# Rows of x instead of table rows for 48 edge tiles, edge lists read in rows, and expert tiles among the last blocks' and the last routing's products

## The chip, the cores and the metric

One Trainium2 chip, one core. Its engines run side by side, each with a queue of its own that is worked off in order: PE (TensorE, matrix products and transposes), DVE (VectorE), ACT (ScalarE), POOL (GpSimd, here almost only the issuer of indirect DMAs) and SP (SyncE, here only an issuer of DMAs). Sixteen DMA engines carry all transfers. The metric is the device time of one execution in microseconds (us); a program's time is the median of several. PE's clock is throttled: the profile shows the granted clock as a share of the full one.

## The reference

A graph layer with attention and then a layer of experts, over N = 6250 nodes of C = 256 numbers and 206,250 edges, sorted by destination. H = 8 heads of D = 32; 16 experts with a hidden layer of 512, two of them for each node.

```
hn    = layernorm(x)                       # no scale, no shift
hh    = (hn @ W).reshape(n, 8, 32)
s     = leaky_relu(<hh, a_src>[src] + <hh, a_dst>[dst])
alpha = softmax of s over the edges of one dst
out   = segment_sum(hh[src] * alpha, dst) + hn
x1    = x + elu(layernorm(out) * gamma + beta)
y     = layernorm(x1)
z     = y + sum over the top 2 of softmax(gate) * expert(y)   # relu, 256 -> 512 -> 256
x2    = x1 + layernorm(z) * gamma2 + beta2
```

Everything is float32 but for a few tables of scores in bfloat16.

## The kernel before

Nodes lie in NB = 49 blocks of 128. Edges lie in NK = 52 windows of CT = 31 tiles of 128 edges, 1612 tiles; a window is worked in four groups of 8, 8, 8 and 7 tiles (`GROUPS`), 208 groups.

**Preparation.** All of x is loaded into `xs` on SP (batches of 2, 6, 8, 8, ... blocks), then the first destination of each window (`base_i`) and the two edge lists `dst_i` and `src_sb`, in which a partition holds 31 successive edges of each window (124 bytes in a piece, `edge_list`, L129). For each block, statistics on DVE (`stats`, L193 and L194), two transposes on PE (L294) copied by ACT (L296), two passes of two products with `wx` (L299; the 256 columns of W and 16 of scores) into one of four PSUM buffers `ph`, and three activations (L302, L308, L309) make a row of R = 280 numbers for each node: eight heads of 32 with a 1 behind each, and 16 exponentials of scores. DVE copies the scores (L310), and the row goes to the DRAM tensor `table` by a DMA that POOL issues (L313). Ahead of batch 6, `windows()` (L242 to L282) makes each edge's destination relative to its window (`dl`), stores it as bytes in rows (`dlb`), and takes its largest and smallest (L271, L272).

**Main loop.** For each group, `gather` (L200) issues one indirect DMA on POOL for each tile (L205): 128 rows of the table by the sources in one column of `src_sb`, into one of four `hx` buffers. `look` (L1022, L1029, L1040) builds on DVE the one-hot matrices of the group one ahead and on PE the destinations' scores. DVE then weighs the rows (L1064, L1067, L1069 and L1072, the long one), and PE adds them up by destination into `agg` (L1076). At a window's end `agg` and a carry from the window before (L1093) are copied and stored to `accd`. When a block's edges are all in, `node_block` (called by `blocks`) reads it back, divides, normalises, and finds the two experts of each node, with PE's share at L623 and L628.

**Experts.** Blocks are routed in five rounds that end at 14, 26, 35, 43 and 49 blocks. `routing` (L634) counts and places the round's nodes and finds the expert of each tile of 128 rows (`owner`, L808). `scatter` (L817, L820, L830) sends each block's rows twice, by two indirect DMAs on POOL, from five buffers `ys`. The round's tiles (43, 39, 33, 31 and 27, together 173) then go through `stages()` (L976), one call per group: it takes a third tile's output (`rows_out`, L896, L898), a second's hidden layer (`hidden`, L881, L890), another's transposes (`turned`, L872, L874) and a next one's weights (`weights`, 512 KB each of w1 and w2 on SP). `some()` issues four scatters and one `stages()`.

**After the loop.** Three sets of buffers take result rows (`fetch_set`, L915), `blocks(summed)` runs the last two node blocks and the last routing, all left scatters go out, and a loop of `stages()` and `result` (L927 to L942) finishes the tiles and the output.

The order of work on each engine is the order in which the program issues it. `tc.issue_after(i)` adds that an instruction stands behind `i` where both are on one engine; across engines it adds nothing. The loop's core:

```
hx, gathered = early.pop(0) if early else gather(k, g0, n)
...
sums.append(t)
some()
if g0 == 0:
    blocks(summed)
    summed = []
```

Of the kernel before, what the change touches and what calls it, by code (L numbers as in the profile page):

```python
# [10 lines left out]
F32 = mybir.dt.float32  # L11
BF16 = mybir.dt.bfloat16
U8 = mybir.dt.uint8
I32 = mybir.dt.int32
# [22 lines left out]
def kernel(  # L37
# [89 lines left out]
    tp, tr = tail // CT, tail % CT  # L127

    def edge_list(eng, t, ap):  # L129
        eng.dma_start(  # L130
            t[:, : (NK - 1) * CT].rearrange("p (k g) -> p k g", g=CT),
            ap[0 : (NK - 1) * CE].rearrange("(k p g) -> p k g", p=P, g=CT),
        )
        o = (NK - 1) * CE
        if tp:
            eng.dma_start(t[:tp, (NK - 1) * CT : NT], ap[o : o + tp * CT].rearrange("(p g) -> p g", g=CT))
        if tr:
            eng.dma_start(
                t[tp : tp + 1, (NK - 1) * CT : (NK - 1) * CT + tr],
                ap[o + tp * CT : NE].rearrange("(p g) -> p g", p=1),  # L140
            )

    hxp = ctx.enter_context(tc.tile_pool(name="hxp", bufs=4))
    prep = ctx.enter_context(ExitStack())
    ed = prep.enter_context(tc.tile_pool(name="ed", bufs=1))
    dst_i = ed.tile([P, NT], I32, name="dst_i")
    nc.vector.memset(dst_i[:, (NK - 1) * CT :], N - 1)
    nc.vector.memset(src_sb[:, (NK - 1) * CT :], PADN)
    nc.vector.memset(src_sb[:, NT:], PADN)
    xs = ed.tile([P, NB, C], F32, name="xs")  # L150
    nc.vector.memset(xs[:, NB - 1, :], 0.0)
    batches = []
    while not batches or batches[-1][1] < NB:
        i = batches[-1][1] if batches else 0
        batches.append((i, min(NB, i + (2, 6, 8)[min(2, len(batches))])))
    for i, j in batches:
        n = min(j, NB - 1) - i
        if n:
            nc.sync.dma_start(xs[:, i : i + n, :], x[i * P : (i + n) * P, :].rearrange("(i p) c -> p i c", p=P))
    nc.sync.dma_start(xs[:LAST, NB - 1, :], x[(NB - 1) * P : N, :])  # L160
    wx = ed.tile([P, KC, C + 2 * H], F32, name="wx")
# [6 lines left out]
    nc.sync.dma_start(base_i[:, : NK - 1], dst[0 : (NK - 1) * CE].rearrange("(k e) -> e k", e=CE)[0:1, :])  # L168
    nc.sync.dma_start(base_i[:, NK - 1 :], dst[(NK - 1) * CE : (NK - 1) * CE + 1].rearrange("(k e) -> e k", e=1))
    edge_list(nc.sync, dst_i, dst)  # L170
    edge_list(nc.sync, src_sb, src)

# [5 lines left out]
    gg = row_of(g_gamma, C, "gg")  # L178
    gb = row_of(g_beta, C, "gb")
    fg = row_of(f_gamma, C, "fg")  # L180
    fb = row_of(f_beta, C, "fb")
    gtb = row_of(gate_b, E, "gtb")
    gw = const.tile([P, KC, E], F32, name="gw")
    nc.sync.dma_start(gw, gate_w.rearrange("(k p) e -> p k e", p=P))


    rest = const.tile([P, NB, C], F32, name="rest")
# [12 lines left out]
    def gather(k, g0, n):  # L200

        hx = hxp.tile([P, n, R], F32, name="hx")
        for g in range(n):
            c = k * CT + g0 + g
            t = nc.gpsimd.indirect_dma_start(  # L205
                out=hx[:, g, :],
                out_offset=None,
                in_=table[:, :],
                in_offset=bass.IndirectOffsetOnAxis(ap=src_sb[:, c : c + 1], axis=0),
            )  # L210
        return hx, t
# [5 lines left out]
    with tc.tile_pool(name="a1", bufs=1) as a1, tc.tile_pool(name="a3", bufs=3) as a3, tc.tile_pool(  # L217
        name="aps", bufs=4, space=bass.MemoryType.PSUM
    ) as aps:
# [22 lines left out]
        def windows():  # L242

            base_f = a1.tile([1, NK], F32, name="base_f")
            nc.vector.tensor_copy(base_f, base_i)
            bb = aps.tile([P, NK], F32, name="pxt")
            nc.tensor.matmul(bb, lhsT=ones[:1, :], rhs=base_f, start=True, stop=True)
            base_b = a1.tile([P, NK], F32, name="base_b")
            nc.vector.tensor_copy(base_b, bb)
            nc.vector.tensor_sub(down[:, : NK - 1], base_b[:, : NK - 1], base_b[:, 1:])  # L250
            nc.vector.tensor_copy(dl, dst_i)
            d3 = dl.rearrange("p (k g) -> p k g", g=CT)
            nc.vector.tensor_tensor(d3, d3, base_b[:, :, None].to_broadcast([P, NK, CT]), ALU.subtract)

            dlt = a1.tile([P, TR, P], U8, name="dlt")
            for i in range(TR):
                n = min(P, NT - i * P)
                pt = aps.tile([P, P], F32, name="pxt")
                nc.tensor.transpose(pt[:n, :], dl[:, i * P : i * P + n], ident)
                nc.scalar.copy(dlt[:n, i, :], pt[:n, :])  # L260
                nc.sync.dma_start(dlb[i * P : i * P + n, :], dlt[:n, i, :])
# [8 lines left out]
            two = a1.tile([P, 2], F32, name="two")  # L270
            nc.vector.tensor_reduce(two[:, 0:1], dl, AX.X, ALU.max)  # L271
            nc.vector.tensor_reduce(two[:, 1:2], dl, AX.X, ALU.min)  # L272
            nc.vector.tensor_scalar(two[:, 1:2], two[:, 1:2], -1.0, float(P - 1), op0=ALU.mult, op1=ALU.add)
            pw = aps.tile([2, P], F32, name="pxt")
            nc.tensor.transpose(pw, two, ident)
# [7 lines left out]

        for q, (i0, i1) in enumerate(batches):
            if q == 6:
                base_f, pf_ = windows()
            for b in range(i0, i1):
                stats(a3, xs[:, b, :], st[:, b, :])
            inv_std(rstd[:, i0:i1], st[:, i0:i1, 1])
            nc.vector.tensor_scalar_mul(low[:, i0:i1], rstd[:, i0:i1], 0.2)  # L290
            for b in range(i0, i1):
                pt = aps.tile([P, KC, P], F32, name="pxt")
                for k in range(KC):
                    nc.tensor.transpose(pt[:, k, :], xs[:, b, k * P : (k + 1) * P], ident)  # L294
# [18 lines left out]
                nc.gpsimd.dma_start(table[b * P : (b + 1) * P, :], hr)  # L313


# [78 lines left out]

    def load(ap, lo_, hi_, engines=mybir.ALL_ENGINES, after=()):


        with ExitStack() as order:
            for i in after:
                order.enter_context(tc.issue_after(i.ins))  # L400
            return nc.values_load(ap, engines=engines, min_val=lo_, max_val=hi_)


    with tc.If(load(flag[:, 0:1], 0, 1) > 0):
        with tc.tile_pool(name="m1", bufs=1) as m1, tc.tile_pool(name="m2", bufs=2) as m2, tc.tile_pool(
# [6 lines left out]
            nc.vector.tensor_copy(dst_f[:, :NT], dst_i)  # L412
# [148 lines left out]
    with tc.tile_pool(name="w2", bufs=2) as w2_, tc.tile_pool(name="w3", bufs=3) as w3_, tc.tile_pool(  # L561
# [22 lines left out]
        def node_block(b):  # L584
# [37 lines left out]
            for k in range(KC):  # L622
                nc.tensor.transpose(pt[:, k, :], y[:, k * P : (k + 1) * P], ident)  # L623
# [3 lines left out]
            for k in range(KC):  # L627
                nc.tensor.matmul(pl, lhsT=yt[:, k, :], rhs=gw[:, k, :], start=(k == 0), stop=(k == KC - 1))  # L628
# [3 lines left out]
            nc.vector.max_index(i8[:, b, :], v8[:, b, :], lg)  # L632

        def routing(i):  # L634
# [48 lines left out]
            for t, m in ((place, tri), (own, ones)):  # L683
                pk = wk.tile([P, nb * E], F32, name="pt")
                nc.tensor.matmul(pk, lhsT=m, rhs=flat, start=True, stop=True)
                nc.scalar.copy(t.rearrange("p b e -> p (b e)"), pk)
# [110 lines left out]
            if not flush:  # L797
# [7 lines left out]
                nc.vector.tensor_copy(opened, tiles_to[:, E - 1 :])  # L805
            po = wk.tile([1, mt], F32, name="pt")
            nc.tensor.matmul(po, lhsT=whose, rhs=take, start=True, stop=True)
            marks["dve"] = nc.vector.tensor_scalar_min(owner[i], po, float(E - 1))  # L808

        scattered = [[] for _ in ROUNDS]  # L810
# [3 lines left out]
        def to_send(b):  # L814

            y = e2.tile([P, C], F32, name="ys", bufs=5)
# [159 lines left out]
        def some():  # L976
            scatters(4)
            stages()
# [65 lines left out]

        weighed = []
# [5 lines left out]
        for k in range(NK):  # L1051
            after = used[-2] if k > 1 else ()
            agg = wps.tile([P, RA], F32, name="agg")
            for g0, n in BOUNDS:
# [4 lines left out]
                hx, gathered = early.pop(0) if early else gather(k, g0, n)  # L1059
# [24 lines left out]
                some()  # L1084
# [40 lines left out]
        blocks(summed)  # L1125
# [56 lines left out]
```

## Time and profile before

| | us |
|---|---|
| median of 7 runs | 2570.33 |
| lowest and highest | 2563.16, 2574.28 |
| the profiled execution | 2565.48 |
| its span | 2563.7 |
| busy in the span: PE, DVE, ACT, POOL | 1832.3, 1608.8, 527.7, 1764.4 |
| first table gather issued | 90.59 |
| first gather of result rows | 2238.34 |
| last window's last sums end | 2254.7 |
| last routing's `owner` | 2291.83 |
| final results | 2531 to 2558 |

The profile is of one execution. A row of the costliest groups gives the line, engine and operation, the tiles written and read, the count, then busy time and mean nanoseconds of one, then the idle time of that engine just before these instructions and what ended it ("issue": nothing that the profile shows). The granted clock over the span was 0.862; the mean traffic 221 GB/s, 567.74 MB in all.

### The profile page before, as it was taken

The numbers are of one execution on the slowest core, as the hardware profiler recorded it, in microseconds if no ns is written. First come the engines' busy times: TensorE is split into PE (matmuls) and PEld (weight loads), VectorE is DVE, ScalarE is ACT, GpSimd is POOL, SyncE is SP. The second block draws the span as 40 slices with busy tenths as digits, with TensorE's granted clock in tenths as the row PEclk, the third lists the DMA queues.
The fourth block names the chain that finished last, engine by engine and source line by source line (L and its number), as shares of the span: only waits on it lengthen the run. The fifth ranks groups of instructions, "written<-read, shape, count | busy, mean of one in ns | idle before, by whom it ended". The sixth has DMA issues, their size and how long they took to land.

```text
span 2563.7 us, 34571 instructions
## 1 busy us (share of the span) xinstructions
PE 1832.3 (71%) x10229; PEld 1541.6 (60%) x10229; DVE 1608.8 (63%) x3120; ACT 527.7 (21%) x1822; POOL 1764.4 (69%) x1866
## 2 busy tenths in 40 slices
PE   7365555555563679889848889876888868868995
PEld 6254444444442568778737778766777657756774
DVE  5476766666664676776746776765776737747702
ACT  6200000000001122222211222212222112224442
POOL 3577777777777777777777777777777777747202
PEclk9687787878876889899969899888999889979997
DMA  8555555555445588898857888877889768959995
GB/s 222 131 154 172 151 161 172 153 170 141 131 137 156 157 251 270 265 288 260 272 172 229 252 282 259 271 242 245 273 273 292 232 216 271 283 166 333 295 293 165
DMA packets 389306, 567.74 MB, mean 221 GB/s; under 512 B 102535, under 2 KB 278750, under 8 KB 389110
## 3 DMA queue, kind: packets, MB, share of 16 engines
q0 software_dynamic: 89904, 263.85, 34.2%
q1 hardware_dynamic: 257130, 264.89, 33.7%
q10 hardware_dynamic: 42076, 36.71, 4.2%
q8 instruction: 84, 1.38, 0.2%
q14 instruction: 112, 0.92, 0.1%
HBM read 497.58 MB, written 67.67 MB: 220 GB/s over the span
## 4 chain that ended last, share of the span: by engine, by line
PE 28%; POOL 21%; DMA 19%; DVE 13%; issue 12%; ACT 1%; DVEq 0%; POOLq 0%; ACTq 0%; SPq 0%
POOL hx L205 20%; PE agg L1076 13%; DMA hx<-table,src_sb 10%; PE po L896 6%; PE ph L881 6%; DVE hx L1072 4%; DMA out_dram<-o 3%; DMA xg<-ys,pos 2%; DMA accd<-carry 2%; DMA a<-accd 1%; DVE oh L1029 1%; POOL xg L830 1%; DVE uv L1067 1%; PE pt L872 1%; ACT hT L890 1%
## 5 line engine op out<-in xcount | busy, mean ns | idle before, releaser
L205 POOL DMA_INDIRECT hx<-table,src_sb x1612 | 1541.8, 956 | 497.9 <-issue 435.3
L1076 PE MATMUL agg<-hx,oh 128*128 128x264 f32 x3224 | 950.0, 451 | 416.7 <-DVE hx L1072 416.6
L1076 PEld LDWEIGHTS agg<-hx,oh 128*128 128x128 f32 x3224 | 689.6, 223 | 555.8 <-DVE hx L1072 430.1
L1072 DVE TENSOR_TENSOR hx<-hx,pm 128x2112 f32<-128x2112 f32 x208 | 474.5, 2281 | 4.2
L896 PE MATMUL po<-w2s,hT 128*128 128x256 f32 x1384 | 356.0, 397 | 86.8 <-ACT hT L890 86.5
L881 PEld LDWEIGHTS ph<-xt,w1s 128*128 128x128 f32 x2768 | 344.9, 195 | 22.7 <-issue 7.6
L881 PE MATMUL ph<-xt,w1s 128*128 128x128 f32 x2768 | 351.2, 280 | 3.8 <-ACT xt L874 2.5
L896 PEld LDWEIGHTS po<-w2s,hT 128*128 128x128 f32 x1384 | 267.3, 199 | 139.0 <-ACT hT L890 101.4
L1029 DVE TENSOR_TENSOR oh<-along,dl 128x1024 f32<-128x1024 f32 x208 | 245.8, 1182 | 22.2 <-PE agg L1076 22.2
L1022 DVE TENSOR_TENSOR ohT<-dlr,along 128x1024 bf16<-128x1024 uint8 x208 | 244.9, 1177 | 0.1
L890 ACT ACTIVATE hT<-ph,b1s 128x128 f32<-128x128 f32 x692 | 200.4, 367 | 215.6 <-PE ph L881 191.7
L1067 DVE TENSOR_TENSOR uv<-uv,hx 128x128 f32<-128x128 f32 x208 | 60.3, 290 | 275.0 <-DMA hx<-table,src_sb 245.0
L915 POOL DMA_INDIRECT hx<-yg,pos x98 | 97.3, 993 | 174.0 <-DVE y L933 141.3
L1064 DVE TENSOR_REDUCE uv<-pm 128x128 f32<-128x384 f32 x208 | 111.3, 535 | 79.6 <-PE pm L1040 77.4
L197 ACT ACTIVATE mv<-mv,eps 128x1 f32<-128x1 f32 x98 | 28.8, 294 | 629.0 <-DVE mv L194 629.0
L830 POOL DMA_INDIRECT xg<-ys,pos x98 | 97.3, 993 | 54.2 <-issue 45.4
L898 ACT COPY yr<-po 128x256 f32<-128x256 f32 x173 | 63.8, 369 | 338.7 <-PE po L896 312.7
L1040 PEld LDWEIGHTS <-ohT 128*128 128x128 bf16 x1612 | 71.3, 96 | 75.7 <-issue 33.8
L1040 PE MATMUL pm<-abw,ohT 128*128 128x48 bf16 x1612 | 74.8, 184 | 55.7 <-DVE ohT L1022 55.7
L874 ACT COPY xt<-pt 128x256 f32<-128x256 f32 x173 | 66.5, 385 | 156.5 <-PE pt L872 156.5
L594 DVE TENSOR_SCALAR den<-a 128x8 f32<-128x8 f32 x49 | 9.3, 190 | 139.0 <-DMA a<-accd 139.0
L817 DVE SCALAR_TENSOR_TENSOR ys<-rest,mv,fb 128x256 f32<-128x256 f32 x49 | 23.7, 484 | 112.1 <-DMA xg<-ys,pos 112.1
(204 smaller groups left out, 1326.2 us busy)
## 6 DMA issues: line engine op xcount, KB each, us to landing
w1s<-in_L_ffn_w_dram SPq DMA_DIRECT2D x173, 512.0 KB
w2s<-in_L_ffn_w_dram SPq DMA_DIRECT2D x173, 512.0 KB
hx<-table,src_sb POOLq DMA_INDIRECT x1612
dlr<-dlb SPq DMA_DIRECT2D x52, 496.0 KB
xr<-xg SPq DMA_DIRECT2D x173, 128.0 KB
yg<-yr ACTq DMA_DIRECT2D x173, 128.0 KB
xg<-zero SPq DMA_DIRECT2D x9, 1024.0 KB
accd<-carry ACTq DMA_DIRECT2D x52, 132.0 KB
```

What stands on the lines that cost most here:

```text
L205: t = nc.gpsimd.indirect_dma_start(out=hx[:, g, :], out_offset=None, in_=table[:, :], in_offset=bass.IndirectOffsetOnAxis(ap=src_sb[:, c : ...
L830: t = nc.gpsimd.indirect_dma_start(out=xg[r][:, :], out_offset=bass.IndirectOffsetOnAxis(ap=pos[k][:n, b : b + 1], axis=0), in_=sent_rows[ ...
L881: marks["pe"] = nc.tensor.matmul(ph[:, f, :], lhsT=w1s[:, k, f * P : (f + 1) * P], rhs=xt[:, k, :], start=(k == 0), stop=(k == KC - 1),)
L890: marks["act"] = nc.scalar.activation(hT[:, f, :], ph[:, f, :], AF.Relu, bias=b1s[:, f : f + 1])
L896: marks["pe"] = nc.tensor.matmul(po, lhsT=hT[:, f, :], rhs=w2s[:, f, :], start=(f == 0), stop=(f == FC - 1))
L915: t = nc.gpsimd.indirect_dma_start(out=into[:n, k, :C], out_offset=None, in_=yg[parts[i][2]][:, :], in_offset=bass.IndirectOffsetOnAxis(ap ...
L1022: nc.vector.tensor_tensor(ohT, dlr[:, g0 : g0 + n, :], along[:, None, P:].to_broadcast([P, n, P]), ALU.is_equal,)
L1029: nc.vector.tensor_tensor(oh, along[:, None, :P].to_broadcast([P, n, P]), dl[:, k * CT + g0 : k * CT + g0 + n, None].to_broadcast([P, n, P ...
L1040: t = nc.tensor.matmul(pm[:, g * S3 : (g + 1) * S3], lhsT=ohT[:, g, :], rhs=abw, start=True, stop=True)
L1064: nc.vector.tensor_reduce(uv, pm[:, : n * S3].rearrange("p (n t h) -> p n h t", n=n, t=3), AX.X, ALU.add)
L1072: nc.vector.tensor_tensor(rows, rows, wt.unsqueeze(3).to_broadcast([P, n, H, D1]), ALU.mult)
L1076: t = nc.tensor.matmul(agg, lhsT=oh[:, g, :], rhs=hx[:, g, :RA], start=(g0 == 0 and g == 0), stop=(carry is None and g0 + g == CT - 1),)
```

## The change

Three parts.

- **Edge lists and preparation.** `src` and `dst` are read as rows, a window to a partition, two halves each, into the four `hx` buffers. `turn_src` turns them on PE into the layout of `src_sb`; a tile is now 128 successive edges. `windows()` works on the rows: it subtracts each window's first destination into `away`, stores all bytes at once, and takes the largest and smallest; after the table's loop `away` is turned into `dl`. x comes in batches into three buffers, each load behind the first table store of the batch two before, and table stores are issued by SP. Six constants are loaded later.
- **Raw tiles.** For the first tile of each of the groups 4 to 51 (windows 1 to 12), 48 in all, the rows of x themselves are gathered into `rest` (which holds nothing yet) ahead of the table's gathers. In the loop these groups gather one tile fewer from the table, and `raw_stats`, `raw_turn` and `raw_rows` make the table's row of that tile from x, as the preparation does for a block. Gathers are issued for the group two ahead, after the group's sums in the program.
- **End.** The last window's groups 2 and 3 have no `some()`. After the loop, three calls of `stages()`, then one behind each of the last two node blocks, two inside the last routing, and one behind it. `ys` has three buffers.

```diff
+    HALVES = ((0, 16), (16, CT))
+    def edge_rows(ap, pad):
+        out = []
+        for lo, hi in HALVES:
+            t = hxp.tile([NK, (hi - lo) * P], I32, name="hx")
...
+            nc.sync.dma_start(t[:split], full[:split])
+            nc.sync.dma_start(t[split : NK - 1], full[split:])
...
-    def gather(k, g0, n):
+    RAW = 48
+    RAW0 = len(GROUPS)
...
+    def gather(k, g0, n, raw=False):
         hx = hxp.tile([P, n, R], F32, name="hx")
-        for g in range(n):
+        for g in range(int(raw), n):
+            t = fetch_rows(hx[:, g, :], table, k * CT + g0 + g)
...
+        def x_rows(q):
+            i, j = batches[q]
+            t = ax.tile([P, 8, C], F32, name="xs")
...
+                if q > 2:
+                    order.enter_context(tc.issue_after(stores[batches[q - 2][0]].ins))
...
+        def turn_src(gs):
...
+                    nc.vector.tensor_copy(
+                        sf[:, done : done + len(here), :], src_r[h][:, here[0] : here[-1] + 1 : d, :]
+                    )
...
+            for i in range(len(gs)):
+                nc.tensor.transpose(pt[:, i, :], sf[:, i, :], ident[:NK, :NK])
+            nc.vector.tensor_copy(
+                src3[:, :, gs[0] : gs[-1] + 1 : d].rearrange("p k g -> p g k"), pt
+            )
...
+            for i, n in enumerate(GROUPS):
...
+                nc.vector.tensor_copy(part, dst_r[h][:, o : o + n, :])
+                nc.vector.tensor_scalar(part, part, first, None, op0=ALU.subtract)
+                nc.vector.tensor_copy(dlt[:, g0 : g0 + n, :], part)
+                for j, op in enumerate((ALU.max, ALU.min)):
+                    nc.vector.tensor_reduce(spread[:, i, j : j + 1], part, AX.XY, op)
+            nc.sync.dma_start(dlb[: NK * CT, :].rearrange("(k g) e -> k g e", g=CT), dlt)
...
+        turn_src(firsts)
+        rest = const.tile([P, NB, C], F32, name="rest")
+        for j in range(RAW):
+            k, i = divmod(RAW0 + j, len(GROUPS))
+            fetch_rows(rest[:, j, :], x, k * CT + firsts[i])
         for q, (i0, i1) in enumerate(batches):
+            if 2 <= q < 6:
+                g0 = firsts[q - 2]
+                turn_src(list(range(g0 + 1, g0 + GROUPS[q - 2])))
...
-                nc.gpsimd.dma_start(table[b * P : (b + 1) * P, :], hr)
+                stores[b] = nc.sync.dma_start(table[b * P : (b + 1) * P, :], hr)
+                if b == i0 and 0 < q < len(batches) - 2:
+                    x_rows(q + 2)
+        for i, n in enumerate(GROUPS):
...
+                nc.tensor.transpose(pt[:, g, :], away[:, g0 + g, :], ident[:NK, :NK])
...
-            y = e2.tile([P, C], F32, name="ys", bufs=5)
+            y = e2.tile([P, C], F32, name="ys", bufs=3)
...
+        def raw_stats(k):
+            js = [g - RAW0 for g in range(k * len(GROUPS), (k + 1) * len(GROUPS)) if g in raws]
+            if js:
+                st = raw_st[:, js[0] : js[-1] + 1, :]
+                for j in js:
+                    stats(w2_, rest[:, j, :], raw_st[:, j, :])
+                inv_std(st[:, :, 0], st[:, :, 1])
+                nc.vector.tensor_scalar_mul(st[:, :, 1], st[:, :, 0], 0.2)
+        def raw_turn(g):
+            pt = wk.tile([P, KC, P], F32, name="pt")
+            for k in range(KC):
+                nc.tensor.transpose(pt[:, k, :], rest[:, g - RAW0, k * P : (k + 1) * P], ident)
+            xt = e2.tile([P, KC, P], F32, name="xt")
+            nc.scalar.copy(xt, pt)
+            turned_rows[g] = xt
+        def raw_rows(g):
...
+            for k in range(KC):
+                nc.tensor.matmul(ph, lhsT=xt[:, k, :], rhs=wx[:, k, :], start=(k == 0), stop=(k == KC - 1))
+            r1, r2 = raw_st[:, g - RAW0, 0:1], raw_st[:, g - RAW0, 1:2]
+            by_head = hx[:, 0, :RA].rearrange("p (h d) -> p h d", h=H)
+            nc.vector.memset(by_head[:, :, D:], 1.0)
+            nc.scalar.activation(
+                by_head[:, :, :D], ph[:, :C].rearrange("p (h d) -> p h d", h=H), AF.Copy, scale=r1
+            )
+            nc.scalar.activation(hx[:, 0, RA : RA + H], ph[:, C : C + H], AF.Exp, scale=r1)
+            nc.scalar.activation(hx[:, 0, RA + H :], ph[:, C : C + H], AF.Exp, scale=r2)
...
-                some()
+                if k < NK - 1 or g0 < GROUPS[0] + GROUPS[1]:
+                    some()
+                with ExitStack() as order:
+                    order.enter_context(tc.issue_after(sums[-1].ins))
+                    order.enter_context(tc.issue_after(weighed[-1].ins))
+                    if g0 == 0:
+                        raw_stats(k + 1)
+                    if now + 2 < NK * len(GROUPS):
+                        ahead(now + 2)
+                    if now + 2 in raws:
+                        raw_rows(now + 2)
+                    if now + 3 in raws:
+                        raw_turn(now + 3)
...
-        blocks(summed)
+        def more(n):
+            for _ in range(n):
+                with tc.issue_after(chain[-1].ins if chain else sums[-1].ins):
+                    stages()
+        chain = [sums[-1]]
+        more(3)
+        for b in summed:
+            chain.append(node_block(b, [marks["pe"].ins]))
+            more(1)
...
+        routing(len(parts) - 1, lambda: more(2))
+        more(1)
         scatters(len(scat))
```

## Prediction

> **What bounds the kernel now.** I read the page's costliest groups first, then the waits of POOL over the main loop, then the busy times by stretch. The page:
>
> ```profile
> L205 POOL DMA_INDIRECT hx<-table,src_sb x1612 | 1541.8, 956 | 497.9 <-issue 435.3
> L1072 DVE TENSOR_TENSOR hx<-hx,pm 128x2112 f32<-128x2112 f32 x208 | 474.5, 2281 | 4.2
> L817 DVE SCALAR_TENSOR_TENSOR ys<-rest,mv,fb 128x256 f32<-128x256 f32 x49 | 23.7, 484 | 112.1 <-DMA xg<-ys,pos 112.1
> ```
>
> One row says what the loop is paced by: 1612 table gathers of 956 ns, and 435.3 us of idle time ahead of them that is "issue", so POOL waited for nobody. What it does wait for, 126 to 2240 us (releaser: total us, times, longest):
>
> ```profile
> POOL hx L205 <- issue: 428.3, 1406, 0.3
> POOL hx L205 <- PE agg L1076: 18.3, 60, 0.3
> POOL hx L205 <- DMA hx<-table,src_sb: 12.2, 27, 4.3
> ```
>
> 428.3/1406 = 0.30 us, and the waits put down to PE are of that same 0.3 us: they are the gap under another name. A gather thus costs 0.956 + 0.30 = 1.25 us. Check: the timeline has the first table gather at 90.59 and the first gather of results at 2238.34 us; 1612 gathers and 86 scatters in between, 1698 x 1.25 = 2122 of 2147.75 us. The loop is POOL's. Whether the others would let it go faster is read from the stretches without expert tiles, and the ends from those around the loop (us; busy us and count of PE, PEld, DVE, ACT, POOL; granted clock, DMA share, GB/s):
>
> ```profile
> 20.00:40.00 20.00, 19.07 (x96) 15.57 (x96) 19.07 (x108) 17.58 (x73) 8.64 (x16) 1.00 1.14 257
> 40.00:60.00 20.00, 18.75 (x94) 15.17 (x93) 4.96 (x69) 16.45 (x66) 8.15 (x17) 1.00 0.47 148
> 60.00:80.00 20.00, 17.64 (x86) 13.64 (x85) 8.68 (x23) 13.35 (x55) 5.90 (x11) 0.91 0.35 93
> ...
> 300.00:400.00 100.00, 56.54 (x265) 45.08 (x266) 70.75 (x115) 7.10 (x21) 75.79 (x80) 0.83 0.54 153
> ...
> 2265.00:2292.00 27.00, 5.16 (x18) 3.55 (x18) 16.96 (x82) 4.95 (x17) 2.61 (x3) 0.60 0.28 98
> 2292.00:2320.00 28.00, 24.44 (x122) 19.29 (x122) 15.37 (x44) 9.45 (x39) 21.32 (x20) 0.84 0.72 226
> 2320.00:2445.00 125.00, 111.62 (x625) 89.86 (x625) 94.84 (x262) 59.63 (x234) 53.75 (x55) 0.96 0.98 312
> 2445.00:2528.00 83.00, 74.75 (x485) 66.09 (x485) 0.00 (x0) 34.47 (x112) 0.00 (x0) 1.00 0.93 290
> ```
>
> Three regimes: a preparation paced by PE (19 of 20 us busy), a loop paced by POOL with DVE at 71 and PE at 57 per 100 us, and a tail paced by DMA (0.93 to 0.98), with a hole at 2265 to 2292 us where DMA is at 0.28 while the last two node blocks and the last routing run.
>
> **Part 1: 48 raw tiles (term -60).** In windows 1 to 12 each group takes its first row tile from `rest`, so POOL issues 7, 7, 7, 6 gathers instead of 8, 8, 8, 7. 48 x 1.25 = 60 us leave POOL's loop; the 48 x-row gathers stand on POOL ahead of the table. What replaces them, per raw tile: DVE one bn_stats and one aggregate (0.40 + 0.16 by L193, L194), a memset and a share of the window's scale, together some 0.8; PE two transposes and four matmuls, by L294 and L299 (14.5/98, 49.8/196 busy) 0.30 + 1.02 = 1.3 at clock 1.0, 1.6 at 0.8; ACT one copy and three activations, by L296, L302, L308, L309 0.39 + 0.48 + 0.27 + 0.28 = 1.4. A group of 8 takes 8 x 1.25 = 10 us now and would take 8.75. DVE has 7.1 + 0.8 = 7.9 of it, PE 5.7 + 1.6 = 7.3, ACT 0.7 + 1.4: all fit, DVE closest at 90%. The hx ring has four buffers, so gathers may be three groups, 26 us, ahead of the sums that free them: a DVE delay of a few us is absorbed. The program also puts a group's four scatters behind two later groups of gathers rather than one, which can only shorten POOL's waits on DVE; 2147.75 - 2122 = 26 us of waits are all there is to win. Bounds: -75 (with half of these) to -35 (DVE at 90% passes on half a microsecond per group).
>
> **Part 2: preparation (term +14).** Removed: the edge lists in 124-byte pieces, the strained stretch at 20 to 40 us (share 1.14), and part of the windows step, which held the first blocks back 69.75 to 76.99. Added on PE: 31 source transposes and 31 of `away`, by L259 at most 0.31 each but smaller, say 0.15: 4.7 us before and about 2 on the chain behind the blocks. Added on DVE, in program order between the score copies (L310) of blocks 5 and 6: batch 2's statistics (8 x 0.57), the source copies, and cast, subtraction, cast and two reductions over 52 x 3968 elements, which by L271 (1612 elements in 1.82 us) and L251 (1.00) come to about 11 us; 17 to 18 us in all. PE may run four `ph` buffers ahead, 4 x 1.27 = 5 us, so it stands still for some 12. Against that 2 to 3 us from the shorter chain in windows and a few from the edge rows. 5 + 12 + 2 - 5 = +14: the first table gather at about 105 instead of 90.6. The raw gathers need the turned source list, at about 26 us; 48 x 1.25 + 3 of ramp ends at 89, so the table covers them: with the table at 105 by 16 us, and with one at 90.6, as now, still by 1.6; only a source list later than 28 us would show. Table stores move to SP, in line with the x loads: a load waits behind the first store of the batch two before, some 20 us ahead of its use. Bounds: 0 (DVE's block falls into waits it has anyway: it is only 25% busy at 40 to 60) to +45 (the traffic: 48 x 128 rows of 1 KB are 6.3 MB, with 7 MB of table and 5 of x 18 MB between 26 and 90; at the rate that 148 GB/s at a share of 0.47 makes for a share of one, 315 GB/s, that is 58 us, but at the 172 GB/s of the page's best early slice it is 106).
>
> Here a rule speaks against the change. The Trainium skill (DMA: Bandwidth & Descriptors, Issuing engines are not separate DMA queues) says that transfers started by any engine end on the same 16 DMA engines, so that POOL's idle time is no idle time of theirs and moving the stores to SP buys no bandwidth. The rows of this case leave room after 40 us (shares 0.47, 0.35); by the rule alone a saturated preparation would add the upper bound rather than the term.
>
> **Part 3: the tail (term -22).** Two stages in the last window are left out and eight are put among node blocks 47 and 48 and the routing: six tiles more before the routing's scatters. A tile is 4.24 us in the pure stretch (share 0.93). The hole holds 27 x (1 - 0.28) = 19 us of idle DMA, its neighbours 28 x 0.28 = 8 more; six tiles need 6 x 4.24 = 25. I take 22, since the carry goes out 3.6 us earlier (its PE step no longer stands behind a stage) but the routing's PE steps now stand behind stages that wait for weights, in order, about 6 us later at its end. Bounds -30 and 0 (weights late, routing late by as much as is won).
>
> **Part 4: ys with three buffers (term +3).** DVE waited 112.1 us in 23 waits for scatters with five. Three blocks' scatters last 3 x 2.5 = 7.5 us on POOL, and a buffer comes back 2.4 (landing) + 0.5 + 0.5 after its pair was issued: POOL needn't wait. Where gathers lie between, DVE waits longer, up to a group, inside the slack above. Bounds 0 and +25 (six us at each of four lumps).
>
> Constants loaded later and `base_i` computed lie off every chain: they are needed after the first node block, at 220 us.
>
> **Sum.** -60 + 14 - 22 + 3 = -65 on the profiled 2565.48 us (span 2563.7) is 2500; that execution lies 4.85 below the median 2570.33, so the forecast is 2505 for the median.
>
> **Rivals.**
> 1. The table comes late by DMA and DVE together, at 140 instead of 105 us: +45 in place of +14, 2505 + 31 = 2536. For: three flows in one stretch, DVE in order. Against: the shares after 40 us.
> 2. Loop not POOL's once shortened: DVE at 90% or the ring gives half back, +30: 2535; all, 2565. For: 7.9 of 8.75 us. Against: no wait for DVE over 0.3 us today.
> 3. The tail fill wins nothing: 2527. For: it is DMA work in any case; against: the hole.
> 4. Slower: the three ys buffers put a real POOL wait in every block's scatters. Place: L817 and the scatters, 43 blocks in the loop. Price: landing and refill, up to 3.4 us each, 146 us: 2505 + 143 = 2648. It decides from (2575 - 2505 + 3)/43 = 1.7 us a block. For: 112 us of DVE waits with five. Against: the 7.5 us above, and POOL's scatters wait 4.9 us in all for earlier ones today.
> 5. The change doesn't do what it says: the raw tiles' x rows are still gathered on POOL after the table would be ready; then the 60 us return, 2565.
>
> **How the numbers follow.** Forecast (2475 to 2525) 0.54; rival 1 0.14; rivals 2 and 3 0.08 each; rival 4 0.08; rival 5 0.03; more than bounds allow for, below 2475, 0.05. Range 2468 to 2550: it takes in rivals 1, 3 and the half of 2, and leaves rival 4 and the tails. A measurement of this kernel tells about 0.2%, 5 us, from no change. Faster: all but rival 4, 5 and the whole of rival 2, 0.86; same 0.03; slower 0.11 (rival 4 and pairs of the others, such as 1 with the whole of 2).
>
> **What would show it.** Part 1: gathers from the table 1564, POOL waits of them still 0.3 us, first gather to first result gather about 2148 - 60 = 2088 us. Part 2: the first table gather at 100 to 110; a PE gap of 12 us in blocks 6 to 10. Part 3: DMA share of the hole above 0.8. Part 4: L817's waits above 112, but none of POOL on ys. Wrong would be: a POOL wait of whole microseconds in windows 1 to 12, a first table gather after 140, or the last routing ending more than 10 us later after the last sums.

## The result and the profile after

| | before | after |
|---|---|---|
| median, us | 2570.79 (36 runs) | 2557.62 (15 runs; 2550.75 to 2563.69) |
| ratio to before, 95% interval | | 0.9951 [0.9941, 0.9961] |
| span of the profiled execution | 2563.7 | 2557.5 |
| first table gather | 90.59 | 119.93 |
| first gather of results | 2238.34 | 2230.37 |
| loop: from the one to the other | 2147.75 | 2110.44 |
| tail: from there to the end of the span | 325.4 | 327.1 |

The kernel became faster by about 13 us where 65 were forecast. The three stretches of the table say where to look: the table came 29.3 us later, the loop took 37.3 us less, the tail 1.8 us more, and the spans differ by -6.2.

The costliest groups of after, with the same columns as before:

```profile
L183 POOL DMA_INDIRECT hx<-table,src_sb x1564 | 1495.9, 956 | 530.6 <-issue 417.7
L1206 DVE TENSOR_TENSOR hx<-hx,pm 128x2112 f32<-128x2112 f32 x208 | 474.6, 2282 | 4.1
L906 DVE SCALAR_TENSOR_TENSOR ys<-rest,mv,fb 128x256 f32<-128x256 f32 x49 | 23.8, 487 | 153.7 <-DMA xg<-ys,pos 152.9
```

Exactly 48 gathers are gone, and each costs what it did, 956 ns. But the idle time ahead of the gathers is 530.6 us, of which only 417.7 is "issue"; before it was 497.9 with 435.3. Of the rest, 28.7 us is POOL's wait ahead of the first table gather, its raw gathers being done. And DVE waits 152.9 us for a free `ys` buffer instead of 112.1. What POOL waits for in the loop, 126 to 2240 us (total us, times, longest):

```profile
POOL hx L183 <- issue: 416.5, 1367, 0.3
POOL hx L183 <- PE agg L1210: 24.7, 50, 6.8
POOL hx L183 <- PE pm L1129: 14.5, 8, 12.4
POOL hx L183 <- DMA hx<-table,src_sb: 11.1, 23, 4.4
```

Two longest waits stand out of the 0.3 us that are only the issue gap: 6.8 for the sums and 12.4 for the destinations' scores (`pm`). Before, both rows had no wait of over 1.1 us; the 4.4 of the last row was there with 4.3. The busy times by stretch, of after (us; PE, PEld, DVE, ACT, POOL; granted clock, DMA share, GB/s):

```profile
20.00:40.00 20.00, 16.31 (x83) 12.43 (x82) 10.01 (x35) 10.39 (x41) 8.25 (x8) 1.00 0.47 138
40.00:60.00 20.00, 10.20 (x35) 7.92 (x35) 19.08 (x45) 7.01 (x29) 15.32 (x15) 0.66 0.75 234
60.00:80.00 20.00, 15.74 (x76) 12.59 (x75) 11.15 (x52) 12.52 (x51) 15.25 (x16) 0.91 0.84 257
...
300.00:400.00 100.00, 72.22 (x363) 58.11 (x364) 79.39 (x162) 20.00 (x72) 75.64 (x80) 0.88 0.57 167
2254.00:2276.00 22.00, 8.98 (x60) 7.70 (x58) 5.87 (x20) 6.70 (x23) 5.09 (x6) 0.77 0.69 233
2276.00:2300.00 24.00, 19.69 (x106) 16.85 (x107) 11.28 (x63) 8.06 (x29) 0.01 (x1) 0.85 0.46 141
```

In the raw windows POOL issues its 80 gathers per 100 us as before, while DVE has risen from 71 to 79 and PE from 57 to 72: the loop there is still POOL's. From 40 to 60 us PE is at 10 of 20, where it was at 18.75, and DVE is full. In the tail the hole is still there: DMA at 0.46 from 2276 to 2300.

Three places in the traces show what stands still. First, PE in the preparation of after (start, duration, idle before and its releaser):

```profile
49.05 6.45 PE L349 MATMUL ph<-wx,xt 128*128 128x272 f32 x16 [11.83 <-DVE sd L360]
...
56.69 3.93 PE L349 MATMUL ph<-wx,xt 128*128 128x272 f32 x16 [0.75 <-ACT xt L346]
```

PE waits 11.83 us for a score copy behind `windows()` on DVE. The 16 products after it (four blocks' worth) take 6.45 us; the next 16 take 3.93.

Second, the start of the loop in after. SP's wait from the view of waits, SP's load from the timeline, then POOL's wait:

```profile
SPq L1083 <- DMA hx<-table,src_sb: 15.8, 1, 15.8
```

```profile
154.88 0.37 SPq L1083 DMA_DIRECT2D abw<-abd  x1
```

```profile
175.71 0.94 POOL L183 DMA_INDIRECT hx<-table,src_sb  x1 [12.36 <-PE pm L1129]
```

SP's first load of the loop (`abw`, L1083) waits 15.8 us until the gathers issued ahead of the loop have landed, and goes out at 154.88, 35 us after the first table gather; before it went out at 109.05, 18.5 us after:

```profile
109.05 0.36 SPq L994 DMA_DIRECT2D abw<-abd  x1
```

The destinations (`dlr`), the one-hot matrices, PE's `pm` and the sums that free `hx` follow it, and POOL stands still for 12.36 us.

Third, near the end of the loop, DVE and then POOL in after:

```profile
2069.58 0.55 DVE L906 SCALAR_TENSOR_TENSOR ys<-rest,mv,fb 128x256 f32<-128x256 f32 x1 [19.02 <-DMA xg<-ys,pos]
...
2086.88 0.48 DVE L906 SCALAR_TENSOR_TENSOR ys<-rest,mv,fb 128x256 f32<-128x256 f32 x1 [8.35 <-DMA xg<-ys,pos]
```

```profile
2101.57 0.98 POOL L183 DMA_INDIRECT hx<-table,src_sb  x1 [6.76 <-PE agg L1210]
2133.66 0.94 POOL L183 DMA_INDIRECT hx<-table,src_sb  x1 [3.35 <-PE agg L1210]
```

DVE waits 19.02 us for one buffer of `ys` and soon after 8.35 for another, and everything queued behind them comes later; POOL then waits 6.76 us for an `hx` buffer, a window later 3.35. The long wait alone isn't new. Before had it too, with five buffers, but none of over 2.1 us behind it at this place, and no POOL wait:

```profile
2086.32 0.54 DVE L817 SCALAR_TENSOR_TENSOR ys<-rest,mv,fb 128x256 f32<-128x256 f32 x1 [19.39 <-DMA xg<-ys,pos]
```

### The profile page after: what moved, and what is told of

It is laid out like the page before. It is cut to its first block, busy times and chain, and to the rows that moved or that the text cites. A ratio compares the mean times of both kernels' runs of the same rounds, so it can differ in the third digit from the quotient of the medians.

```text
span 2557.5 us, 35763 instructions
## 1 busy us (share of the span) xinstructions
PE 1879.1 (73%) x10567; PEld 1582.0 (62%) x10567; DVE 1645.6 (64%) x3307; ACT 583.9 (23%) x2029; POOL 1739.6 (68%) x1817
## 4 chain that ended last, share of the span: by engine, by line
PE 24%; DMA 20%; POOL 17%; issue 12%; DVE 12%; ACT 2%; DVEq 0%; ACTq 0%; SPq 0%; POOLq 0%
POOL hx L183 15%; PE agg L1210 11%; DMA hx<-table,src_sb 10%; PE po L985 6%; PE ph L970 5%; DVE hx L1206 4%; DMA out_dram<-o 3%; DMA accd<-carry 2%; DMA a<-accd 2%; DMA xg<-ys,pos 2%; POOL xg L919 1%; DVE uv L1201 1%; DVE oh L1118 1%; DVE uv L1198 1%; ACT hT L979 1%
## 5 line engine op out<-in xcount | busy, mean ns | idle before, releaser
L183 POOL DMA_INDIRECT hx<-table,src_sb x1564 | 1495.9, 956 | 530.6 <-issue 417.7
L1210 PE MATMUL agg<-hx,oh 128*128 128x264 f32 x3224 | 924.7, 443 | 313.4 <-DVE hx L1206 310.5
L1210 PEld LDWEIGHTS agg<-hx,oh 128*128 128x128 f32 x3224 | 677.6, 219 | 447.3 <-DVE hx L1206 323.9
L906 DVE SCALAR_TENSOR_TENSOR ys<-rest,mv,fb 128x256 f32<-128x256 f32 x49 | 23.8, 487 | 153.7 <-DMA xg<-ys,pos 152.9
L702 PE MATMUL pt<-ident,y 128*128 128x128 f32 x98 | 24.7, 342 | 96.4 <-DVE pm L1203 50.5
```

The lines of the kernel that those rows point to most:

```text
L183: return nc.gpsimd.indirect_dma_start(out=out, out_offset=None, in_=table_[:, :], in_offset=bass.IndirectOffsetOnAxis(ap=src_sb[:, c : c + ...
L1210: t = nc.tensor.matmul(agg, lhsT=oh[:, g, :], rhs=hx[:, g, :RA], start=(g0 == 0 and g == 0), stop=(carry is None and g0 + g == CT - 1),)
```

## The experiments

All kernels compute the whole reference. Each ratio is to the kernel before on the same chip.

**1. Only the three buffers.** The kernel before with one number changed:

```diff
-            y = e2.tile([P, C], F32, name="ys", bufs=5)
+            y = e2.tile([P, C], F32, name="ys", bufs=3)
```

> The kernel before with three ys buffers instead of five, nothing else. Theory: with three buffers DVE stops in the lumps of scatters long enough that POOL's gathers wait for hx buffers, and the last routing's owner comes late; the changed kernel's trace shows POOL waits of 6.8 and 3.3 us at the last lump and an owner 6 us behind its ys. So 5 to 15 us slower than before, with POOL waits on PE agg of whole microseconds. Rival (the prediction's working: three blocks' scatters outlast the return of a buffer): within 4 us of before.

Measured: 2586.21 us, 1.0057 [1.0044, 1.0071]. The trace has the table at 88.65, a loop of 2157.23 (+9.5) and a tail of 338.1 (+12.7). One line of POOL's waits in the loop shows the new kind of wait (total, times, longest):

```profile
POOL hx L205 <- PE agg L1076: 25.1, 66, 5.3
```

It stands 13 us behind a second wait of DVE for `ys`:

```profile
2106.12 0.48 DVE L817 SCALAR_TENSOR_TENSOR ys<-rest,mv,fb 128x256 f32<-128x256 f32 x1 [8.48 <-DMA xg<-ys,pos]
```

```profile
2119.16 0.98 POOL L205 DMA_INDIRECT hx<-table,src_sb  x1 [5.27 <-PE agg L1076]
```

So this part alone costs some 14 us by the medians and 20 in the traces. Of the loop's 9.5 us this wait is 5.3; the rest isn't split further. Of the tail's 12.7, 7.9 is that the last sums end 24.2 us behind POOL's first gather of results instead of 16.3: the `hx` buffers let POOL run ahead, so that its loop shows only a part of DVE's and PE's delay. From the last sums to `owner` nothing changes (36.5 against 37.1), and from there to the end it takes 5.5 longer.

**2. After with the old end.** The loop's last groups keep `some()`, and the calls of `stages()` among the last blocks are taken out:

```diff
-                if k < NK - 1 or g0 < GROUPS[0] + GROUPS[1]:
-                    some()
+                some()
...
-        chain = [sums[-1]]
-        more(3)
-        for b in summed:
-            chain.append(node_block(b, [marks["pe"].ins]))
-            more(1)
...
-        routing(len(parts) - 1, lambda: more(2))
-        more(1)
+        blocks(summed)
```

> The changed kernel with the end of the kernel before: some() in all groups, blocks, routing, then scatters, no stages among them. Theory from the two traces: the new end wins nothing, since the node blocks' reads stand behind weights on SP and their PE steps behind stages; so within 6 us of the changed kernel (2557), first scatter of the last round 10 to 15 us earlier against the first gather of results. Rival (the prediction): 22 us slower than the changed kernel, about 2580.

Measured: 2568.62, 0.9983 [0.9973, 0.9993]: 8 us above after by the ratios, 11 by the medians. Its loop is as long as after's (2111.47 against 2110.44), its tail 338.5 instead of 327.1. The new order is thus worth 8 to 11 us: more than nothing, about half of the 22 forecast. Behind `owner` the new order wins much more, 29.0 us (248.3 from `owner` to the end against 277.3 here), and the last sums end 6.1 sooner behind POOL's loop, but `owner` comes 58.6 us after them instead of 34.9 here. That after's tail is nevertheless no shorter than before's comes from experiment 1's 12.7.

**3. After without raw tiles.**

```diff
-    RAW = 48
+    RAW = 0
```

> The changed kernel with no raw tile (RAW = 0): all 1612 tiles from the table, no x rows gathered ahead. Theory: 48 gathers of 1.25 us come back into POOL's loop, +60, and the table comes 5 to 15 us earlier since x loads and table stores no longer share the DMA engines with 6.3 MB: 2600 to 2615. Rival A (the raw tiles saved much less than 60 in the loop because DVE at 80 per 100 us held the groups): under 2585. Rival B (the late table is all the raw rows' traffic): first table gather at 92 to 98 us and about 2590.

Measured: 2610.64, 1.0148 [1.0133, 1.0164]. The loop is 2169.40, that is 59.0 longer than after's, and the first table gather comes at 112.99 instead of 119.93. So the raw tiles give 59 us in the loop, and their rows cost the table 7. One stretch of this kernel:

```profile
300.00:400.00 100.00, 56.20 (x250) 44.57 (x251) 66.45 (x113) 5.75 (x18) 75.94 (x80) 0.79 0.58 166
```

POOL issues at the same pace with DVE at 66 as with DVE at 79.

**4. After with room ahead of a conditional part.** Ahead of the loop the program has a part behind a condition (`tc.If`) for inputs whose windows spread too far; it isn't entered here, and the profile has no line of it. Its pools `m1` and `m2` take memory all the same. In after the loop's pool of `abw` and `dlr` lies at bytes 153824 to 186080 of a partition, across `m1` (146912 to 157312) and `m2` (157312 to 171200); in before it ended below `m1` (151264 to 183520 against 187456). An unused tile of 39 KB pushes them up:

```diff
+        with tc.tile_pool(name="m0", bufs=1) as m0, tc.tile_pool(name="m1", bufs=1) as m1, tc.tile_pool(
...
+            m0.tile([P, 9792], F32, name="room")
```

> The changed kernel with an unused 39 KB pool ahead of the pools of the branch that is never taken (the overflow path behind the flag), so that the loop's pool w3 no longer lies on their memory. Theory: SP's first loop load of abw waits for the landing of all 24 early gathers only because of that overlap; without it the first dlr loads go out some 15 us earlier, POOL's 12.4 us wait for the first buffer goes to 1 or 2 us, and the kernel is 8 to 12 us faster than the changed one: about 2547. Rival (the wait is needed for another reason, or another wait takes its place): within 3 us of 2557.

Measured: 2548.44, 0.9906 [0.9891, 0.9921], below after by 11 us by the ratios and the traces, 9 by the medians. The SP timeline and the POOL timeline of this kernel:

```profile
139.88 0.37 SPq L1086 DMA_DIRECT2D abw<-abd  x1
```

```profile
166.53 0.94 POOL L183 DMA_INDIRECT hx<-table,src_sb  x1 [1.61 <-PE pm L1132]
```

With the table as late as in after (121.22), the load goes out 18.7 us behind it, as in before, and POOL's wait shrinks from 12.36 to 1.61 us.

**5. The same with five buffers again** (room for them by one buffer instead of two for `neg` and `yt`, which this run thus changes as well):

```diff
-            neg = w2_.tile([P, C], F32, name="neg")
+            neg = w2_.tile([P, C], F32, name="neg", bufs=1)
...
-            yt = w2_.tile([P, KC, P], F32, name="yt")
+            yt = w2_.tile([P, KC, P], F32, name="yt", bufs=1)
...
-            y = e2.tile([P, C], F32, name="ys", bufs=3)
+            y = e2.tile([P, C], F32, name="ys", bufs=5)
```

> The kernel of e4_room with five ys buffers again; the 2 KB come from the node block's neg and yt, now one buffer each instead of two. Theory: three buffers cost the kernel before 14 us (9.5 in the loop, the rest after it), so here 12 to 20 us less than e4_room: about 2532, no POOL wait on PE agg over 1 us, and the last owner ahead of its ys. Rival (the new end hides what the old end paid; single neg and yt cost something): at most 8 us less, about 2542.

Measured: 2529.63, 0.9842 [0.9823, 0.9862], 19 us less than experiment 4 by the medians and the traces, 16 by the ratios (the two were timed on different chips). The loop is 2088.74, 11.7 less, the tail 319.8, 5.4 less. POOL's waits and DVE's `ys`:

```profile
POOL hx L183 <- PE agg L1213: 19.2, 62, 0.6
```

```profile
L909 DVE SCALAR_TENSOR_TENSOR ys<-rest,mv,fb 128x256 f32<-128x256 f32 x49 | 23.7, 483 | 114.9 <-DMA xg<-ys,pos 114.8
```

DVE waits 114.8 us, nearly as before, and POOL's longest wait for the sums is 0.6 us.

**6. The same with DVE's work in `windows()` spread** over the copies of the scores, so that these no longer stand behind it (17.6 us in all, 10 of them in one piece ahead of a copy):

```diff
-                nc.vector.tensor_copy(part, dst_r[h][:, o : o + n, :])
+                with tc.issue_after(copied[9 + 8 * i].ins):
+                    nc.vector.tensor_copy(part, dst_r[h][:, o : o + n, :])
...
+                    with tc.issue_after(copied[13 + 2 * j + 8 * i].ins):
+                        nc.vector.tensor_reduce(spread[:, i, j : j + 1], part, AX.XY, op)
...
-                nc.vector.tensor_scalar(sd[:, b, :], ph[:, C:], r1, None, op0=ALU.mult)
+                copied.append(nc.vector.tensor_scalar(sd[:, b, :], ph[:, C:], r1, None, op0=ALU.mult))
```

> e5_ys5 with DVE's work of windows() (casts, subtraction, reductions over the edge rows, 17 us in one piece between the score copies of blocks 5 and 10) laid out behind the score copies of blocks 9 to 39, one piece of 0.7 to 1.2 us at a time. Theory: PE's 11.8 us stop and the slower clock behind it go, the first table gather comes 12 to 16 us earlier than the 121 of e4_room, and the time falls by as much: about 2518. Rival (the late table is held by x loads and table stores beside the raw rows' traffic): at most 5 us, first table gather after 115.

Measured: 2517.86, 0.9789 [0.9771, 0.9807], 12 us less. The first table gather is at 107.31 instead of 119.14. The stretch that showed PE at 10 of 20, in this kernel:

```profile
40.00:60.00 20.00, 17.33 (x80) 13.62 (x79) 15.01 (x55) 14.55 (x58) 15.11 (x17) 0.91 0.99 310
```

PE works on at 17.33 and the DMA share is 0.99: what is left of the lateness lies beside full DMA engines.

**7. The same with the last two blocks' sums read back first.** In after the loads of `a` (L663) stand on SP behind those of the three stages. SP's timeline in after:

```profile
2261.30 0.37 SPq L957 DMA_DIRECT2D w2s<-in_L_ffn_w_dram  x1
2262.57 0.34 SPq L944 DMA_DIRECT2D xr<-xg  x1
2263.16 0.37 SPq L950 DMA_DIRECT2D w1s<-in_L_ffn_w_dram  x1
2263.77 0.34 SPq L952 DMA_DIRECT2D b1s<-b1d  x1
2264.16 0.48 SPq L663 DMA_DIRECT2D a<-accd  x1
2265.82 0.33 SPq L944 DMA_DIRECT2D xr<-xg  x1
2266.20 0.43 SPq L663 DMA_DIRECT2D a<-accd  x1
```

The last carry had been sent to `accd` at 2251.5 (8.5 us earlier than before, 2260.0), yet both loads are out at 2266.20, later than before's at 2265.00. The edit:

```diff
-        more(3)
-        for b in summed:
-            chain.append(node_block(b, [marks["pe"].ins]))
+        read_back = [sums_of(b) for b in summed]
+        with tc.issue_after(read_back[-1][1].ins):
+            more(3)
+        for b, (a, _) in zip(summed, read_back):
+            chain.append(node_block(b, [marks["pe"].ins], a))
```

> e6_spread with the last two blocks' reads of accd put on SP ahead of the three stages after the loop instead of behind their weight loads. Theory: the reads go out as soon as the carry has landed, 5 us after its store, instead of 12.6, and the last routing and its scatters come 6 to 8 us earlier: 4 to 8 us less than e6_spread. Rival (the weights behind the reads are late by as much, and the stretch after is bound by DMA): within 3 us of e6_spread.

Measured: 2503.66, 0.9737 [0.9719, 0.9755], 14 us less by the medians, more than expected. The chain behind the reads gives 10 of it: the last routing's `owner` comes 48.1 us after the last sums where it came 58.3 after them in experiment 6. The span is 11.9 shorter: the last sums end 0.6 earlier, `owner` follows them 10.2 sooner, and the end follows `owner` 1.2 sooner. SP's timeline and the tail's stretches of this kernel:

```profile
2217.06 0.84 SPq L668 DMA_DIRECT2D a<-accd  x2
2218.48 0.40 SPq L968 DMA_DIRECT2D w2s<-in_L_ffn_w_dram  x1
```

```profile
2214.00:2236.00 22.00, 15.87 (x92) 13.74 (x92) 9.03 (x31) 8.29 (x29) 6.34 (x7) 0.92 0.78 246
2236.00:2262.00 26.00, 20.04 (x135) 17.56 (x133) 9.06 (x55) 8.53 (x31) 6.22 (x7) 1.00 0.72 232
```

Here the carry is sent at 2214.7 and the loads follow at 2217.06. The same second stretch in experiment 6, where the carry is sent at nearly the same time (2215.2):

```profile
2236.00:2262.00 26.00, 16.79 (x94) 14.20 (x94) 14.33 (x69) 8.73 (x30) 0.00 (x0) 0.79 0.37 104
```

There the hole had DMA at 0.37, here it has 0.72: nearly the share over 0.8 that the forecast asked for. The tail is 312.4 us, in experiment 6 it was 319.2. The last routing's `owner` in before, after, 6 and 7, in this order:

```profile
2291.83 0.16 DVE L808 TENSOR_SCALAR owner<-pt 1x27 int32<-1x27 f32 x1
```

```profile
2309.21 0.17 DVE L896 TENSOR_SCALAR owner<-pt 1x27 int32<-1x27 f32 x1
```

```profile
2272.64 0.17 DVE L903 TENSOR_SCALAR owner<-pt 1x27 int32<-1x27 f32 x1
```

```profile
2261.87 0.17 DVE L907 TENSOR_SCALAR owner<-pt 1x27 int32<-1x27 f32 x1
```

The last sums end at 2254.7, 2250.6, 2214.4 and 2213.8, so `owner` follows them by 37.1, 58.6, 58.3 and 48.1 us.

**8. The same with the last block's scatters behind the routing on DVE**, since `owner` still stood behind a `ys` wait of 7.8 us:

```diff
-        scatters(len(scat))
+        scatters(len(scat) - 2)
+        with tc.issue_after(marks["dve"].ins):
+            scatters(len(scat))
```

> e7 with the last block's two scatters issued behind the routing's work on DVE instead of ahead of it, so that the owner of the last tiles no longer stands behind the last pair's wait for a ys buffer (7.8 us in e7). My theory: the owner ends 5 to 6 us earlier, the last stages' weights follow, and the time is 3 to 6 us below e7, about 2499. Rival: the weights in front of the owner are what the end waits for, and the last scatters, 7 us later on POOL, hold the last gathers: within 2 us of e7, or above it.

Measured: 2513.93, 0.9770 [0.9749, 0.9791]. The wait is gone (1.5 us) and `owner` came at 2255.99 in this trace, yet the median lies 10 us above experiment 7's, on another chip.

**9. The mended kernel without raw tiles** (experiment 8 with `RAW = 0`).

> e8 with no raw tiles (all 1612 gathers from the table), to price the raw tiles in the mended kernel. My theory (a tile is worth 1.25 us of POOL's issue pace, and the x-row traffic delays the table by about 7 us): loop 60 us longer, table some 7 us earlier, so about 50 to 53 above e8, near 2550. Rival (the mended loop is paced by DVE or PE as well as POOL in the raw windows, or the other repairs had won the same time): less than 40 above e8.

Measured: 2558.86, 0.9956 [0.9941, 0.9972]. By the medians 45 us above experiment 8, by the traces 52.2: the loop 62.2 longer, the tail 4.0 shorter, the table at 99.73 instead of 105.69. That is about what they were worth in after (51 by the ratios of experiment 3, 52.6 by the spans), and not under 40.

**10 and 11. The kernels of 7 and 8 once more, on one chip.**

> The kernel of e7 once more, beside e8's on one chip, since the two were timed on different chips. Theory that moving the last scatters gains nothing that lasts (the traces show an owner 6 us earlier and a tail 4 us shorter in e8, while its median lay 10 us above e7's): the two within 5 us of each other, at 2503 to 2514. Rival (the earlier owner is a real gain or a real loss): e7 over 5 us away from e8.

> The kernel of e8 once more, beside e7's on the same chip. Theory: within 5 us of e7, the profile's tail 3 to 4 us shorter. Rival: 5 us or more below e7 (the owner was worth its 6 us) or 5 us or more above it (the moved scatters cost more than the owner gains).

Measured: 2503.21, 0.9748 [0.9728, 0.9768], and 2503.13, 0.9746 [0.9728, 0.9764]. They are equal: moving the last scatters gains nothing that the medians show. The traces say why 8's earlier `owner` was no evidence: in 11 it came at 2262.58 without any long `ys` wait, and in 10 at 2254.89 with one of 7.43. The last sums had ended at 2218.4 in 11 and at 2206.3 in 10, and `owner` moves with them. Counted from there it came after 48.1 and 48.6 us in 7 and 10, after 47.0 and 44.2 in 8 and 11: where the `ys` wait is gone, `owner` waits 5.2 us for PE instead.

## Why the prediction was wrong, by its steps

All in one table (us, from the traces):

| | first table gather | loop | tail | span |
|---|---|---|---|---|
| before | 90.59 | 2147.75 | 325.4 | 2563.7 |
| after | 119.93 | 2110.44 | 327.1 | 2557.5 |
| 1 before, three `ys` | 88.65 | 2157.23 | 338.1 | 2584.0 |
| 2 after, old end | 118.33 | 2111.47 | 338.5 | 2568.3 |
| 3 after, no raw tiles | 112.99 | 2169.40 | 327.7 | 2610.1 |
| 4 room | 121.22 | 2100.41 | 325.2 | 2546.8 |
| 5 and five `ys` | 119.14 | 2088.74 | 319.8 | 2527.7 |
| 6 and DVE spread | 107.31 | 2090.24 | 319.2 | 2516.7 |
| 7 and reads first | 104.53 | 2087.88 | 312.4 | 2504.8 |
| 10 the same again | 104.19 | 2086.58 | 307.3 | 2498.1 |

**Part 1, -60: right.** 59.0 (experiment 3), 62.2 in the mended kernel (9). 1.25 us a gather holds; rival 2 (DVE or PE takes over) is wrong, POOL's pace in the raw windows is unchanged. Rival 5 is wrong too: the raw gathers run from 29.6 to 90.3 us and have no wait of over 1 us in between.

**Part 2, +14: the size was wrong; +29.3.** The stall was foreseen at 12 us, behind 17 to 18 us of work between two score copies; it was 11.83 behind 17.8 (30.95 to 48.78), and experiment 6 shows that it is worth 12. What failed is the rest, "5 + 12 + 2 - 5": without the stall the table still lay 17 us later than before in experiment 6, 14 in 7, where the step says 2. About 6 to 7 of it comes with the raw rows' gathers (3 and 9), whose traffic the step had at nothing because the shares of before left room after 40 us. The rule that was weighed there, from the Trainium skill (DMA: Bandwidth & Descriptors, Issuing engines are not separate DMA queues), thus had a part of the truth: once the stall is gone, in experiment 6, the share is 0.99 at 310 GB/s from 40 to 60 us. The 315 GB/s worked out for a share of one was good, and the upper bound of 106 us, built on 172 GB/s, too pessimistic; 172 isn't the best early slice of before's page either, as the first has 222. In after DVE waits 9.2 us in three waits for rows of x, and ACT 4.1 once for a table store; how the remaining 7 to 10 us (experiment 9, with neither stall nor raw rows, still has 9.1) divide among these, the turns of the lists and the credit for edge rows was not tried. Rival 1, a late table, thus came in part: 15 of its 31 us, about 7 of them with the raw rows (its 2536 us goes with a table at 136 us; one at 140 makes 2540).

**A term that was missing: +11.** The sum let the loop start behind the table as it had. In after its first load waited for the gathers ahead of it, since memory that had been its own now lay where the conditional part's pools lie. Experiment 4 moved those pools and nothing else: the wait and 11 us went. That the overlap makes the wait is what this edit shows; which instruction of that part it goes back to stays open. The prediction named the sign, "a POOL wait of whole microseconds in windows 1 to 12", but had no cause for it: it read the diff's queues, not where its tiles come to lie.

**Part 4, +3: wrong, about +20.** +9.5 in the loop and +12.7 in the tail (1), and back by 19 (5), inside the bound of 25. The step that failed is "DVE waits longer, up to a group, inside the slack above". The longest wait, of 19 us and more, was there with five buffers and no POOL wait followed it; with three, a second of over 8 us stands close behind it, and the two together are more than the ring absorbs. And the term ended with POOL's loop, though DVE and PE come out of it 7.9 us further behind POOL, and the last routing with them. Rival 4 had the place, but not the form: two POOL waits of 6.76 and 3.35 us, not 43.

**Part 3, -22: half of it came, -11.** The step said that the carry goes out 3.6 us earlier and that the routing's end comes about 6 later. The carry went out 8.5 us earlier, 4.4 of it against the last sums, so this was right. The step that failed is the 6: `owner`, near the last routing's end, came 21.5 us later after the last sums than before (58.6 against 37.1), and so the prediction's own sign of being wrong, over 10 us, was met. 10 us of it stands on SP: the three stages' weights were issued ahead of the reads of `accd`, so that the early carry lay unread. With the reads first (7) `owner` follows the last sums by 48.1, and the tail is 13.0 us shorter than before's, 18.0 in the repeat (10), all with five buffers. That doesn't reach the 22, and the other 11 us by which `owner` is late are not gone: the two stages inside the routing lie there, and in 8 and 11 `owner` waits for PE, but no run took these stages alone out. Rival 3 (nothing) is wrong.

**The sum.** Measured piece by piece: -59 + 29 + 11 - 11 + 22 = -8, where the traces of before and after differ by -6.2. So nothing large is left over. Experiment 7's kernel comes near to the forecast by its three stretches: first table gather at 104.53 (forecast 105), a loop 60 shorter (57), a tail 13 shorter (22), 2503 us (2505). This is in part luck: the mended kernel has five `ys` buffers and not three, and in the table the stall, the largest term, is gone and the traffic and waits stand in its place.

Experiment 7's kernel is faster than both: 0.9737 and, repeated, 0.9748 of the time before, some 67 us.

## What to carry over

Walk every queue that a moved step passes, SP's above all: here three stages' weight loads put ahead of two small reads took back 10 us of the tail's gain. Fewer buffers were paid for neither at the mean wait nor at the longest one, which five buffers had too, but at the next wait behind it and at the end of the loop, where the delay that the ring had hidden from POOL came out. And when a stretch is measured from one engine's last step, see how far the other engines are behind it: here from 14 to 26 us, as much as the gains in question. When pools change size, look at where every tile of the next phase now lies, also against parts of the program that never run: the waits come with the memory.

## What the runs showed of the hardware

After the 11.83 us in which PE stood still in after, 16 products took 6.45 us instead of 3.93; the granted clock in the profile was 0.63 from 49 to 56 us and 1.00 from 56 to 60. These products thus lost 2.5 us beside the stall. But the table came no more than 11.83 us earlier without it (6), where 16 products at 45.59 us still took 5.48 at a clock of 0.71, after a wait of 1.45 us.

With gathers of x rows, loads of x and table stores together, the DMA engines carried 310 GB/s at a share of 0.99 (experiment 6, 40 to 60 us).
